# A fused linear layer with mean and condition terms on one core: first loads over one queue, tiles 4 to 7 turned by VectorE, bias added as banks are emptied, half the turned chunks in SBUF

## The chip, the cores and the metric

The kernel runs on one core of one Trainium2 chip. The time is device microseconds from start to end of one execution. Engines are named as in the profile: PE (TensorE, the matrix products), PEld (its weight loads), DVE (VectorE), ACT (ScalarE), POOL (GpSimd), SP (SyncE, which here only issues DMAs). A name with a q behind it (SPq, POOLq) is that engine's instruction queue.

## What is computed

The layer takes rows of x, the mean of x over the sequence and a condition vector used twice, multiplies all of them by one weight matrix, adds a bias, applies relu and adds x again. Shapes: x is (4, 1024, 512), the condition (4, 256), W (1536, 512), b (512), all float32.

```python
def _L0_cond_ref(hidden0, hidden1, x, W, b):
    hidden = jnp.concatenate([hidden0, hidden1], axis=-1)      # (B, 512)
    x_mean = jnp.mean(x, axis=1, keepdims=True)                # (B, 1, 512)
    ones_L = jnp.ones((1, L, 1), dtype=x.dtype)
    fused = jnp.concatenate([x, x_mean * ones_L, hidden[:, None, :] * ones_L], axis=-1)
    return jax.nn.relu(jnp.einsum('bld,do->blo', fused, W) + b)
x = x + _L0_cond_ref(cond_512, cond_512, x, L0_cond_W, L0_cond_b)
```

Only the x part of `fused` differs from row to row. The mean part and the condition part are the same for all 1024 rows of one batch entry, so the kernel computes them once per entry, together with b, as one 512-wide "bias".

## The kernel before

**Tiles.** The output has 32 tiles of 128 rows by 512 columns: eight tiles per batch entry r (the code calls an entry a row), numbered t = 0 to 31. One tile is one PSUM bank. Its product needs x with the contraction dimension on the partitions, so x is transposed ("turned") in chunks. The contraction of 512 is split into four parts j of 128.

**Three passes per product.** TensorE multiplies fp32r operands. To keep float32 accuracy, each turned chunk is split into a high part `hi` (ScalarE, L265, which also sums the chunk for the mean) and a low part `lo` (VectorE, L281); W is split in the same way into `w_hi` (L233) and `w_lo` (L235). `product(t, j)` (L459) issues three matrix products of 128 x 512: hi by w_hi, hi by w_lo, lo by w_hi. A tile takes 12 of them. The last tile is done in two halves of 256 columns, so that its second half overlaps the first one's end.

**Turning.** `units` (L156) groups tiles: tile 0, tile 1, tiles 2 and 3, tiles 4 to 7, then groups of four. Groups 0 to 3 (`TURN_PE`, the first entry) are turned by TensorE with an identity (L252) from x as loaded for the residual (L178). All later groups are turned by VectorE in 32 x 32 blocks (L254): the DMA brings x a second time as `z` (L191), four strided loads of 256 KB per group, laid out so that the block transposes give the full transpose. One piece is a group's chunk for one j (tiles 0 and 1: all j in one); there are 34 pieces. Turned pieces go to one of two PSUM banks (`ps_x`), their hi and lo parts to SBUF (`S_BUFS` = 15 pieces).

**The bias of an entry.** Sums over the sequence are added up (L336). Two condition terms are weighed by ScalarE (L348) and added by GpSimd (L353) into `cond`, starting from b times 1024 (L321). VectorE adds four mean terms in turn into `acc` in PSUM (L341), the first from `cond` in SBUF. `acc` is split into hi and lo (L357, L361), and two products with a matrix of 1/1024 (L373) sum over the partitions and spread the bias to all partitions of the bank `pb`.

**Getting the bias into a tile.** There are three ways. Tiles 0 to 2 (`KEEP`) are copied out by ScalarE before the bias is known (L473) and get it later by VectorE (L477). Tiles 3 to 15 (entries below `BY_PE` = 2) get it on TensorE: a product of a 64-row matrix `even` with the split bias `row` (L470) into the tile's bank, after which ScalarE's relu empties the bank (L480). Tiles 16 to 30 get it as VectorE empties the bank (L477), and relu follows in SBUF (L480). The last tile starts each half with two products that put its bias in (L455). GpSimd adds x (L485), and SyncE stores the tile (L497).

**What sets the order.** The schedule is manual. `Plan` holds every step with its cost per engine, its dependencies and an urgency; it places steps one by one at the earliest simulated start, and emits them in that order, so each engine's instruction order is fixed before launch, and an engine that waits holds up everything behind it on its queue. SyncE's loads and stores are in the same plan. The first loads are written out by hand (L198 to L211): x on SyncE, W's first block on ScalarE's queue, the condition and b on GpSimd's. Buffers: five banks for tiles, two for turned pieces, one for bias work; three z groups, four x groups, ten output tiles.

Of the kernel before, what the change touches and what calls it, by code (L numbers as in the profile page):

```python
# [1 line left out]

# [13 lines left out]
N_WARM = 11  # L16


class Plan:
# [5 lines left out]
    HANDOVER = 0.2  # L25
    PATIENCE = 0.1

    def __init__(self, engines):
        self.free = dict.fromkeys(engines, 0.0)
        self.todo, self.done, self.log = {}, {}, []  # L30

    def add(self, key, costs, deps, urgency, emit, later=0.0):


        assert key not in self.todo, key
        self.todo[key] = (costs, list(deps), urgency, emit, later)

    def run(self):
        while self.todo:
            could = []  # L40
            for key, (costs, deps, urgency, _, _) in self.todo.items():
                if not all(d in self.done for d in deps):
                    continue
                options = []
                for engine, cost in costs.items():
                    start = self.free[engine]
                    for d in deps:
                        end, later, by = self.done[d]
                        if by != engine:
                            end += later + self.HANDOVER  # L50
                        start = max(start, end)
                    options.append((start + cost, start, engine, cost))
                _, start, engine, cost = min(options)
                could.append((start, urgency, key, engine, cost))
            assert could, list(self.todo.items())[:8]
            first = min(could, key=lambda t: t[:2])
            start, _, key, engine, cost = min(
                (t for t in could if t[3] == first[3] and t[0] <= first[0] + self.PATIENCE),
                key=lambda t: (t[1], t[0]),
            )  # L60
            _, _, _, emit, later = self.todo.pop(key)
            self.log.append((start, engine, key, start - self.free[engine]))
            self.free[engine] = start + cost
            self.done[key] = (start + cost, later, engine)
            emit(engine)
# [512 lines left out]
```

## Time and profile before

| what | value |
|---|---|
| median of three runs | 117.61 us (117.05 to 119.56) |
| profiled execution: span | 115.7 us |
| moved by DMA | 26.31 MB, mean 227 GB/s (17.83 MB read, 8.39 MB written) |
| queue of SyncE (q1) | 25.17 MB, 75.7% of 16 engines' span |
| queue of ScalarE (q10) | 1.05 MB, 3.1% |

The profile shows one execution. In a timeline line the first number is the start and the second the duration, in us; brackets at its end hold the idle time before the instruction and what ended it. In a line of groups, "x30 | 38.7, 1315 | 38.9 <-ACT o" means 30 instructions, 38.7 us busy, 1315 ns each on average, 38.9 us idle before them, mostly ended by ScalarE's write to o. In the chain in order of time, each line is the start, the duration, the engine, the tile and line, and how many instructions were merged. In a table of stretches each line is the stretch, its length, and for each engine (PE, PEld, DVE, ACT, POOL) busy us and instruction count, then TensorE's granted clock as a share of full speed, the busy share of the DMA engines and GB/s. Matmul durations overlap, since they are pipelined: the spacing of starts is the cost.

### The profile page before, as it was taken

The page shows a single profiled execution, that of the slowest core. Times are in us where ns is not written, and L with a number is a line of the kernel's source. Part 1 is how long each engine was busy: PE and PEld are TensorE (multiplying, and loading weights), DVE is VectorE, ACT ScalarE, POOL GpSimd, SP SyncE. Part 2 cuts the span into 40 slices and gives each one's busy share as a digit, 9 for nine tenths or more (in the row PEclk, how much of TensorE's full clock was granted, in tenths as well). Part 3 has the DMA queues.
Part 4 walks back from the last instruction along what each step waited for, and adds up shares of the span by engine and source line. Part 5 has one row for each costly group of instructions (what it writes and reads, how often), then busy time and mean ns, then how long its engine had stood idle before and what let it go on. Part 6 is the DMA issues. An engine that isn't in the chain of part 4 may idle for free.

```text
span 115.7 us, 1477 instructions
## 1 busy us (share of the span) xinstructions
PE 107.7 (93%) x466; PEld 82.9 (72%) x466; DVE 81.0 (70%) x114; ACT 53.4 (46%) x122; POOL 57.8 (50%) x55
## 2 busy tenths in 40 slices
PE   5926999999999999999999999999999999999980
PEld 2415788888766687877766688887888878888870
DVE  1066734399999999976896999939999980632250
ACT  5055547887568460424963542246466140642200
POOL 6507144899809643040893029508354913199400
PEclk9998599999999999999999999999999999999999
DMA  3799999999999959999959999994422422025351
GB/s 109 179 392 396 394 370 198 203 203 205 205 256 281 199 136 207 304 388 390 349 177 213 272 397 407 400 258 176 164 91 106 169 91 91 0 91 222 140 227 45
DMA packets 22999, 26.31 MB, mean 227 GB/s; under 512 B 1228, under 2 KB 13776, under 8 KB 22864
## 3 DMA queue, kind: packets, MB, share of 16 engines
q1 hardware_dynamic: 22352, 25.17, 75.7%
q10 hardware_dynamic: 576, 1.05, 3.1%
q8 instruction: 3, 0.05, 0.2%
q14 instruction: 4, 0.03, 0.1%
q0 software_dynamic: 64, 0.01, 0.0%
HBM read 17.83 MB, written 8.39 MB: 227 GB/s over the span
## 4 chain that ended last, share of the span: by engine, by line
PE 89%; DMA 7%; SPq 1%; DVE 0%; issue 0%
PE po_None L459 77%; DMA x<-in_x_dram 7%; PE po_None L470 4%; PE xT L252 3%; PE po L459 2%; PE pb L373 2%; SPq L178 1%; PE po L455 0%; DVE o L490 0%; PE pt L324 0%
## 5 line engine op out<-in xcount | busy, mean ns | idle before, releaser
L485 POOL TENSOR_TENSOR o<-o,x 128x512 f32<-128x512 f32 x30 | 38.7, 1315 | 38.9 <-ACT o L480 32.1
L459 PE MATMUL po_None<-w_hi,hi 128*128 128x512 f32 x124 | 50.8, 409 | 0.0
L459 PE MATMUL po_None<-w_lo,hi 128*128 128x512 f32 x124 | 49.4, 398 | 0.0
L459 PE MATMUL po_None<-w_hi,lo 128*128 128x512 f32 x124 | 49.3, 398 | 0.0
L459 PEld LDWEIGHTS po_None<-w_hi,hi 128*128 128x128 f32 x124 | 23.5, 190 | 7.1 <-issue 1.6
L459 PEld LDWEIGHTS po_None<-w_hi,lo 128*128 128x128 f32 x124 | 23.6, 190 | 5.7
L459 PEld LDWEIGHTS po_None<-w_lo,hi 128*128 128x128 f32 x124 | 23.6, 190 | 5.0
L281 DVE TENSOR_TENSOR lo<-xT,hi 128x512 fp32r<-128x512 f32 (+1 forms) x34 | 21.9, 647 | 7.2 <-ACT hi L265 7.2
L254 DVE STREAM_TRANSPOSE xT<-z 128x512 f32<-128x512 f32 x24 | 26.2, 1102 | 0.3
L265 ACT ACTIVATE hi<-xT 128x512 fp32r<-128x512 f32 (+1 forms) x34 | 19.3, 571 | 9.3 <-DVE xT L254 5.5
L477 DVE TENSOR_TENSOR o<-po_None,bias 128x512 f32<-128x512 f32 x15 | 9.8, 677 | 12.2 <-ACT bias L379 4.1
L480 ACT ACTIVATE o<-o 128x512 f32<-128x512 f32 x17 | 10.5, 631 | 7.5 <-DVE o L477 7.5
L480 ACT ACTIVATE o<-po_None 128x512 f32<-128x512 f32 x13 | 7.5, 601 | 7.9 <-PE po_None L470 7.9
L341 DVE SCALAR_TENSOR_TENSOR acc<-w_mean,tot,acc 128x512 f32<-128x512 f32 x12 | 9.1, 756 | 0.4
L252 PE MATMUL xT<-ident,x 128*128 128x128 f32 x32 | 6.0, 307 | 3.5 <-DMA x<-in_x_dram 3.5
L252 PEld LDWEIGHTS xT<-ident,x 128*128 128x128 f32 x32 | 5.1, 207 | 4.6 <-issue 2.5
L357 ACT ACTIVATE acc_hi<-acc 128x512 fp32r<-128x512 f32 x4 | 2.4, 600 | 11.9 <-DVE acc L341 11.9
L265 ACT ACTIVATION_READ_ACCUMULATOR hi<-xT 128x1 f32 x32 | 6.4, 201 | 0.0
L353 POOL TENSOR_TENSOR cond<-bL,term 128x512 f32<-128x512 f32 x4 | 5.2, 1303 | 2.0 <-ACT term L348 2.0
L341 DVE SCALAR_TENSOR_TENSOR acc<-w_mean,tot,cond 128x512 f32<-128x512 f32 x4 | 5.7, 1426 | 0.6 <-POOL cond L353 0.3
L348 ACT ACTIVATE term<-wc,cT 128x512 f32<-128x512 f32 x8 | 5.6, 723 | 0.7 <-POOL cond L353 0.7
L353 POOL TENSOR_TENSOR cond<-cond,term 128x512 f32<-128x512 f32 x4 | 5.5, 1383 | 0.3
(54 smaller groups left out, 60.7 us busy)
## 6 DMA issues: line engine op xcount, KB each, us to landing
out_dram<-o SPq DMA_DIRECT2D x31, 256.0 KB, 2.4
x<-in_x_dram SPq DMA_DIRECT2D x7, 1024.0 KB, 7.9
z<-in_x_dram SPq DMA_DIRECT2D x24, 256.0 KB, 7.4
w_x<-in_L_cond_W_dram ACTq DMA_DIRECT2D x4, 256.0 KB, 7.2
w_cond<-in_L_cond_W_dram SPq DMA_DIRECT2D x1, 1024.0 KB, 12.7
w_mean<-in_L_cond_W_dram SPq DMA_DIRECT2D x1, 1024.0 KB, 12.6
x<-in_x_dram SPq DMA_DIRECT2D x2, 256.0 KB, 4.1
x<-in_x_dram SPq DMA_DIRECT2D x1, 512.0 KB, 8.0
```

Of the source, the lines that this page charges most:

```text
L252: nc.tensor.transpose(v[:, (m * n + i) * P : (m * n + i + 1) * P], x_t[:, j], ident)
L254: nc.vector.transpose(v[:, : n * P].rearrange("p (n t) -> p n t", t=Q), zs[u].rearrange("p n (a j) -> p n j a", j=J)[:, : n * NQ, js[0], :],)
L265: nc.scalar.activation(hi[c][:, :m], xT[c][:, :m], AF.Copy, accum_out=sums[:, r, js[0], s : s + 1] if len(js) == 1 else None,)
L281: nc.vector.tensor_tensor(lo[c][:, :m], xT[c][:, :m], hi[c][:, :m].bitcast(F32), ALU.subtract)
L341: nc.vector.scalar_tensor_tensor(acc[r], w_mean[:, j, :], totals[r][:, j : j + 1], acc[r] if j else conds[r], ALU.mult, ALU.add,)
L348: nc.scalar.activation(terms[r, k], wc[:, k], AF.Copy, scale=cT[:, k, r : r + 1])
L353: nc.gpsimd.tensor_tensor(conds[r], conds[r] if k else bL, terms[r, k], ALU.add)
L459: nc.tensor.matmul(pos[key][:, :w], lhsT=v[p][:, c], rhs=m[:, j, d], start=(h is None and j == 0 and n == 0), stop=((t < KEEP or r >= BY_P ...
L470: nc.tensor.matmul(pos[t], lhsT=even, rhs=rows[t // NK], start=False, stop=True)
L477: nc.vector.tensor_tensor(o, o if t < KEEP else pos[t], biases[t // NK], ALU.add)
L480: nc.scalar.activation(o_tile(t), pos[t] if KEEP <= t < BY_PE * NK else outs[t], AF.Relu)
L485: nc.gpsimd.tensor_tensor(outs[t], outs[t], x_tile(t), ALU.add)
```

## The change

The text is rewritten, but the tiles, the three passes and the path of the bias up to `pb` stay. What differs:

- **First loads**: SyncE issues all of them, in the order x0, W0, x1, W1, W2, W3, x of tiles 2 and 3, cond, b; `w_cond`, `w_mean`, the z groups and the x groups follow as the planner places them. W's first block uses a buffer of the x pool, which has five now.
- **Turning**: `BY_PE` = (0, 1, 2) now names the groups that TensorE turns, so tiles 4 to 7 are turned by VectorE from four more z loads. For groups that VectorE turns, the pieces of odd j are written to SBUF (`in_sbuf`), those of even j to PSUM as before; the low part of a piece in SBUF may be made by VectorE or GpSimd.
- **Bias**: no bias product per tile. Tiles 0 to 3 (`PARK`) are copied out and get the bias later (VectorE or GpSimd); tiles 4 to 30 get it as VectorE empties the bank; relu follows in SBUF for all of 0 to 29. The last tile starts each half with one 64-row product `preload` instead of two.
- **acc** starts with a ScalarE copy of `cond` into PSUM, so all four VectorE mean terms read `acc` from PSUM. Sums are scaled by 1/1024 in a tiny step of their own; b is no longer scaled.
- **Start of TensorE**: 5 warm-up products in place of 11, and `fill()` products of the same kind wherever the plan shows TensorE idle for over 0.35 us before the condition is turned. For tiles 0 to 3 (`FINE`) each of the three passes is a step of its own; a tile's parts j need only follow its first product, and not one another.
- **Planner**: due times are worked back from wanted ends; a step costs an occupancy and a latency per engine; loads and stores pass through one simulated DMA pipe; 240 noisy orders are simulated and the one with the shortest simulated end is emitted. `S_BUFS` is 14 (was 15), output buffers 12 (was 10).

```diff
-    S_BUFS = 15
-    X_BUFS = 4
-    O_BUFS = 10
-    TURN_PE = (0, 1, 2, 3)
-    BY_PE = 2
-    KEEP = 3
+    S_BUFS = 14
+    X_BUFS = 5
+    O_BUFS = 12
+    N_WARM = 5
+    PARK = 4
+    ALONE = NT - 2
+    FINE = 4
+    SEEDS = 240
...
+    BY_PE = (0, 1, 2)
+    def in_sbuf(c):
+        u, js = pieces[c]
+        return u not in BY_PE and js[0] % 2 == 1
...
+    first_loads = [
+        (("x", 0, 0), MB / 4, lambda e: load_x(0, 0, 1)),
+        (("w", 0), MB / 4, lambda e: load_w(0)),
+        (("x", 0, 1), MB / 4, lambda e: load_x(0, 1, 1)),
+        (("w", 1), MB / 4, lambda e: load_w(1)),
+        (("w", 2), MB / 4, lambda e: load_w(2)),
+        (("w", 3), MB / 4, lambda e: load_w(3)),
+        (("x", 0, 2), MB / 2, lambda e: load_x(0, 2, 2)),
+        (("c",), 0.05, lambda e: nc.sync.dma_start(out=c_sb, in_=cond)),
+        (("b",), 0.05, lambda e: nc.sync.dma_start(out=b_sb[0:1, :], in_=b.rearrange("(o d) -> o d", o=1))),
+    ]
...
     def turn(c):
-        v = xT[c] = ps_x.tile([P, G * P], F32, tag="x", name=f"xT{c}")
-        if u in TURN_PE:
+        if in_sbuf(c):
+            v = xT[c] = spool.tile([P, G * P], F32, tag="xs", bufs=2, name=f"xT{c}")
+        else:
+            v = xT[c] = ps_x.tile([P, G * P], F32, tag="x", name=f"xT{c}")
+        if u in BY_PE:
...
+        plan.add(("lo", c), {"dve": (a, a + 0.06)} | ({"pool": (1.3, 1.35)} if in_sbuf(c) else {}), [("hi", c)],
+                 lambda e, c=c: split_lo(e, c))
...
+    def acc_start(r):
+        acc[r] = ps_b.tile([P, D], F32, tag="b", name=f"acc{r}")
+        nc.scalar.activation(acc[r], conds[r], AF.Copy)
     def mean_term(r, j):
-        if not j:
-            acc[r] = ps_b.tile([P, D], F32, tag="b", name=f"acc{r}")
         nc.vector.scalar_tensor_tensor(
-            acc[r], w_mean[:, j, :], totals[r][:, j : j + 1], acc[r] if j else conds[r],
-            ALU.mult, ALU.add,
+            acc[r], w_mean[:, j, :], totals[r][:, j : j + 1], acc[r], ALU.mult, ALU.add
         )
...
-    def bias_to_bank(t):
-        nc.tensor.matmul(pos[t], lhsT=even, rhs=rows[t // NK], start=False, stop=True)
+    def preload(h):
+        nc.tensor.matmul(bank(LAST, h)[:, :HALF], lhsT=even, rhs=row["v"][:, columns(h)], start=True, stop=False)
...
+        if t < PARK:
+            plan.add(("freed", t), {"act": (0.49, 0.58)}, done + room, lambda e, t=t: keep(t), soft=chain)
+            plan.add(("biased", t), {"dve": (0.62, 0.68), "pool": (1.3, 1.35)}, [("freed", t), ("bias", r)],
+                     lambda e, t=t: add_bias(e, t))
+        elif t < ALONE:
+            plan.add(("freed", t), {"dve": (0.6, 0.66)}, done + room + [("bias", r)],
+                     lambda e, t=t: add_bias(e, t), soft=chain)
...
+    makespan, log, worst, how = plan.search(SEEDS)
+    pe_free, opened = 99.0, True
+    for s, e, key in log:
+        opened = opened and key[0] != "cT_pe"
+        if e == "pe":
+            if opened and s - pe_free > 0.35:
+                for _ in range(int((s - pe_free - 0.1) / 0.22)):
+                    fill()
+            pe_free = s + plan.tasks[key][0][e][0]
+        plan.tasks[key][2](e)
```

More of the change, by code (lines that the diff above doesn't have):

```diff
@@ L15 @@
 PSUM = bass.MemoryType.PSUM
-N_WARM = 11
 class Plan:
[L25 to L39, printed above, removed]
-            could = []
[L41 to L59, printed above, removed]
-            )
[L61 to L65, printed above, removed]
@@ L217 @@
[L217 to L226 removed]
+            deps = []
@@ new lines @@
+                key = ("product", t, j) + (("right",) if h else ())
+                cost = STEP if h is None else STEP / 2
+                plan.add(key, {"pe": (cost, cost + 0.17)},
+                         [("hi", c), ("lo", c), ("w_hi", j), ("w_lo", j)] + (first if not j else []),
+                         lambda e, t=t, j=j, h=h: product(t, j, h=h), due=due(t, j, 0, h or 0),
+                         soft=[key[:2] + (0,) + key[3:]] if j else chain)
+    for t in range(NT):
+        r, k = divmod(t, NK)
+        room = [("stored", t - O_BUFS)] if t >= O_BUFS else []
+        chain = [("freed", t - 1)] if t else []
+        done = [d for j in range(J) for d in made(t, j)]
```

540 lines of the change are left out of this document (304 added, 236 removed).

## The prediction

> **What bounds the kernel now.** I read the page's busy shares first, then the chain of work that ended last, then that chain in order of time, then stretches of the start, and last the queues of VectorE, GpSimd and SyncE.
>
> ```profile
> span 115.7 us, 1477 instructions
> PE 107.7 (93%) x466; PEld 82.9 (72%) x466; DVE 81.0 (70%) x114; ACT 53.4 (46%) x122; POOL 57.8 (50%) x55
> PE 89%; DMA 7%; SPq 1%; DVE 0%; issue 0%
> ```
> The chain is TensorE for 89% of the span: from its first product to its last no other engine holds the end. So an edit is worth what it takes out of TensorE's row of work, or out of the time before that row begins. The chain in order of time, then TensorE's timeline around one bias product:
>
> ```profile
> 15.37 0.71 PE xT L252 x6
> 17.48 0.47 PE xT L252 x4
> ...
> 33.34 0.90 PE po_None L470 x3
> 34.23 1.60 PE po_None L459 x6
> 35.83 0.42 PE po_None L470
> ...
> 54.35 1.35 PE po_None L470 x5
> ...
> 76.44 21.69 PE po_None L459 x93
> 98.13 0.45 PE pb L373 x2
> ...
> 112.40 0.02 issue
> 112.42 0.42 DVE o L490
> ```
> ```profile
> 38.86 0.40 PE L459 MATMUL po_None<-w_hi,lo 128*128 128x512 f32 x1
> 39.19 0.50 PE L470 MATMUL po_None<-row,even 64*128 64x512 f32 x1
> 39.62 0.50 PE L459 MATMUL po_None<-w_hi,hi 128*128 128x512 f32 x1
> 39.96 0.40 PE L459 MATMUL po_None<-w_lo,hi 128*128 128x512 f32 x1
> ```
> A product of 512 columns costs 21.69/93 = 0.233 us, a transpose 0.47/4 = 0.117. A bias product standing alone costs more than a product: from 38.86 to 39.96 lie two products and one bias product, so it takes 1.10 - 2 x 0.233 = 0.63 us, since TensorE loses time on both sides of the 64-row operand. The end is 112.42, and 3.3 us follow it (a VectorE step and the last store).
>
> The start, by stretches of 5 us (their last columns are granted clock, DMA share, GB/s), then its timeline:
>
> ```profile
> 0.00:5.00 5.00, 3.81 (x12) 1.59 (x13) 0.35 (x3) 1.49 (x2) 3.38 (x13) 1.00 0.50 122
> 5.00:10.00 5.00, 1.52 (x11) 1.17 (x10) 2.67 (x5) 2.23 (x4) 1.11 (x1) 1.00 1.03 378
> 10.00:15.00 5.00, 5.00 (x20) 3.85 (x20) 3.39 (x8) 2.57 (x8) 1.43 (x2) 0.66 1.07 401
> 20.00:25.00 5.00, 5.00 (x25) 4.13 (x24) 3.10 (x4) 4.64 (x10) 4.30 (x4) 1.00 1.22 204
> ```
> ```profile
> 0.74 1.87 SPq L178 DMA_DIRECT2D x<-in_x_dram  x4
> 1.20 3.90 PE L144 MATMUL pw<-warm 128*128 128x512 bf16 x11 [1.20 <-DVE ones L137]
> 4.93 0.64 PE L252 MATMUL xT<-ident,x 128*128 128x128 f32 x4
> 6.66 0.63 ACT L233 ACTIVATE w_hi<-w_x 128x512 fp32r<-128x512 f32 x1 [4.43 <-DMA w_x<-in_L_cond_W_dram]
> 7.20 0.58 ACT L265 ACTIVATE hi<-xT 128x512 fp32r<-128x512 f32 x1
> 7.33 0.69 DVE L235 TENSOR_TENSOR w_lo<-w_x,w_hi 128x512 fp32r<-128x512 f32 x1 [1.02 <-ACT w_hi L233]
> 10.04 0.48 PE L459 MATMUL po_None<-w_hi,hi 128*128 128x512 f32 x1
> 16.00 2.54 POOL L332 TENSOR_TENSOR wc<-w_cond 128x512 f32<-128x512 f32 x2 [3.98 <-DMA w_cond<-in_L_cond_W_dram]
> ```
> The first quarter of W is there only at 6.66 and products begin at 10.04, with x, W and w_cond sharing the transfers. TensorE then stays busy 102.4 us (10.04 to 112.4), of which (1 - 0.66) x 5 = 1.7 us go to a clock granted at half after the sparse stretch before.
>
> **The change part by part.**
>
> *First loads in order of need.* Nine go through SyncE: 256 KB each for x0, W0, x1, W1, W2, W3, then 512 KB of x, then cond and b; w_cond and w_mean come behind. At 1.87/4 = 0.47 an issue, W0's starts at 1.2 as it does now from ScalarE, and the ninth is out by 5.0, ahead of the data; GpSimd's two small issues, now SyncE's, were off the path and stay so. By the rows 0.61 MB have passed at 5.0 and 0.378 MB more in each us after. W0 is complete after 0.52 MB, about 4.4. How late the landing is seen has no row of its own: zero below; above, w_cond's 4.19 MB had passed at about 14.2 and were used at 16.00, so 1.8. I take 0.8, nearer the lower end, as fewer loads run side by side: W0 at 5.2. With 0.63 for w_hi and some 0.15 of handovers, products begin at **6.0** (5.2 with no lag; 7.5 if W0 lands at 6.66 as now).
>
> *New waits there.* W1 (1.05 MB) is seen at 7.0, so its w_hi serves at 7.6. Until then TensorE has three products of tile 0 and four transposes, 1.2 us less their own waits, for 1.6 us: about **0.9** us stand idle (0 to 2), tile 1 being late too. W3 (1.57 MB, 8.3) is usable at 9.7 while TensorE has work until about 12, so it costs nothing. Tile 1's transposes now lie behind the first product: +0.5.
>
> *Five warm-up products for eleven.* 3.90/11 = 0.355 each, so they end near 3. The planner may add some in gaps. The loss to half clock is 1.7 now; it may be 0 or the same 1.7; I take 0.8, between. The Trainium skill, page "TensorE: Matmul & The Clock Gate", section "Part 1: The HAM clock gate", says that the full clock is granted only after a busy window of about 3.4 us. By that rule five would not do, the sum would be 0.9 higher, and the time 109.1, inside the forecast's own range; no run yet shows it.
>
> *Tiles 4 to 7 by VectorE.* Sixteen transposes leave TensorE: -16 x 0.117 = -1.9. Four strided x loads (1.05 MB) are added; the row 20 to 25 shows such loads at 204 GB/s, 5.1 us. Behind 2.1 MB (9.0) they end at 14.1, seen at 14.9; TensorE is busy with tiles 0 to 3 (48 products, 12 transposes) until 6.0 + 0.9 + 0.8 + 11.2 + 1.4 = 20.3, so the first turned chunk (turn 1.1, high part 0.6, low part 0.65, handovers: 2.6, ready at 17.5) has 2.8 us to spare. If w_cond and w_mean go ahead (2.1 MB, 5.3 us), that cover is gone and 2.5 us are lost.
>
> *Bias added as banks are emptied.* The 13 bias products go: five alone at 0.63, the three in 0.90 and the five in 1.35 with about 0.2 behind each group (six products in 1.60 where 1.40 is usual): 3.1 + 1.1 + 1.55 = **-5.8**. For the last tile two 64-row products replace four half ones: between -0.2 and +0.8, I take +0.3. VectorE gets the work:
>
> ```profile
> L321 DVE TENSOR_SCALAR bL<-b_sb 128x512 f32<-128x512 f32 x1 | 0.9, 905 | 0.0
> L485 POOL TENSOR_TENSOR o<-o,x 128x512 f32<-128x512 f32 x30 | 38.7, 1315 | 38.9 <-ACT o L480 32.1
> L254 DVE STREAM_TRANSPOSE xT<-z 128x512 f32<-128x512 f32 x24 | 26.2, 1102 | 0.3
> L281 DVE TENSOR_TENSOR lo<-xT,hi 128x512 fp32r<-128x512 f32 (+1 forms) x34 | 21.9, 647 | 7.2 <-ACT hi L265 7.2
> L477 DVE TENSOR_TENSOR o<-po_None,bias 128x512 f32<-128x512 f32 x15 | 9.8, 677 | 12.2 <-ACT bias L379 4.1
> L341 DVE SCALAR_TENSOR_TENSOR acc<-w_mean,tot,acc 128x512 f32<-128x512 f32 x12 | 9.1, 756 | 0.4
> L341 DVE SCALAR_TENSOR_TENSOR acc<-w_mean,tot,cond 128x512 f32<-128x512 f32 x4 | 5.7, 1426 | 0.6 <-POOL cond L353 0.3
> ```
> VectorE: 81.0 + 4 turns (4.4) + 13 more additions (31 for 18, 8.8) - 4 x 0.67 (ScalarE now writes acc's first term, 2.7) - 1.3 for small ones (bL's scaling and one low part of a bias row, less four scalings of sums) = **90.2**, of which GpSimd can take up to 14 low parts. ScalarE gains about 3 (four first terms and one more copy at 0.6) on 53.4, and has room.
>
> *Half the chunks turned into SBUF.* The turn itself has no row with that target: I take the 1.102 of the turn into PSUM, the same operation. What is new is that their low part reads two SBUF tensors. The timeline shows what such an instruction does beside GpSimd:
>
> ```profile
> 43.18 1.29 POOL L485 TENSOR_TENSOR o<-o,x 128x512 f32<-128x512 f32 x1 [1.49 <-ACT o L480]
> 43.22 1.82 DVE L341 SCALAR_TENSOR_TENSOR acc<-w_mean,tot,cond 128x512 f32<-128x512 f32 x1
> ```
> VectorE's step with w_mean and cond, both in SBUF, takes 1.82, ending 0.57 behind GpSimd's; its twelve sisters with acc in PSUM take 0.756. Over the four the excess is 1.426 - 0.756 = 0.67 each. The change removes these four and brings 14 low parts that VectorE or GpSimd (about 1.3 each) may do. The Trainium skill, page "SBUF — State Buffer", section "Who interferes with whom", says that a VectorE instruction with two SBUF inputs and a GpSimd one that reads SBUF exclude each other for a whole instruction; the trace agrees (1.82 against 0.756), and the rule speaks against this part. At half of them on VectorE: 7 x 0.67 = 4.7, with 7 x 0.65 moved off: VectorE stays near 90 in some 104. No engine exceeds TensorE then, but VectorE's idle share falls from 30% to some 13%. The waits of TensorE that follow have no row: zero below, as now; above, 5 (the second rival's price). I take **1.5**, nearer zero because GpSimd, 50% busy, can take low parts. This is the least certain term.
>
> *New planner.* Each queue still runs one fixed order; SyncE's matters most:
>
> ```profile
> SPq L497 <- POOL o L485: 46.6, 21, 5.5
> 58.48 2.04 SPq L191 DMA_DIRECT2D z<-in_x_dram  x4
> ```
> Stores wait for GpSimd 21 times, 46.6 us, up to 5.5; what stands behind them waits too. The last z group now goes at 58.48, before most stores. With one group more and the same three buffers that order tightens. By bytes it fits: 2.1 MB to 9.0, seven z groups 36, two weight blocks 5.3, four x groups and 16 stores 10.6 each give 71.5, and the last group (tiles 28 to 31) is needed near 84: 103.0 less its four tiles' products 11.2, four turns 4.4 and a bias chain of about 6, plus one tile's 2.8, since the bias frees a bank only for the second of them. I cost it at nothing beyond the 1.5.
>
> **The sum.** TensorE's row: 102.4 - 1.9 - 5.8 + 0.5 + 0.3 - 1.7 + 0.8 + 0.9 + 1.5 = 97.0. From 6.0 it ends at 103.0; with 3.3 behind it the span is 106.3. The profiled execution's 115.7 stands 1.9 below the median 117.61 of the three runs; the same added gives **108.2**.
>
> **The rivals.**
> *Nothing waits.* First product at 5.2, full clock, no idle at the start, none later: 108.2 - 0.8 - 0.8 - 0.9 - 1.5 = 104.2. TensorE's almost gapless row now speaks for it; three queues filled above 80% speak against.
> *VectorE becomes the bound through the shared reading.* All 14 low parts on VectorE at 0.67 extra: 90.2 + 9.4 = 99.6, of which some 6.4 fall before 15 (the rows of the three first stretches); the rest, run without a gap from 15, ends at 108.2, and with 3.3 and 1.9 that is 113.4. That the planner may choose GpSimd speaks against. It is the rule of the Trainium skill's page "SBUF — State Buffer" carried to its end.
> *Slower: loads behind stores.* If SyncE's order puts z groups behind stores that wait for GpSimd, a group comes late by up to the 5.5 shown, and nothing else turns the next chunk. Three late groups not covered by chunks in store give 108.2 - 1.5 + 16.5 = 123.2; it decides from about 4.5 us each (over 120). Speaking against it: up to 14 chunks, over three groups, can be held ahead.
> *The loads gain nothing by their order.* Products begin at 7.5: 109.7, inside the likeliest case's own range.
>
> **How the numbers follow.** 0.47 for the forecast (own range 106 to 110), 0.18 for nothing waits (104 to 106), 0.17 for VectorE as bound (110 to 115.2), 0.07 for a mixture ending within 2% (115.3 to 120, about what a measurement of this kernel can tell from no change), 0.11 for slower, most of it loads behind stores. Faster 0.82, same 0.07, slower 0.11. The range 104.0 to 114.0 leaves out the last two and a little of the third.
>
> **What would show it.** The first product near 6.0 and no half clock beyond 11; no 64-row products before the last tile; the chain still TensorE, in one row of about 97 us; low parts from SBUF on VectorE over 1 us where GpSimd runs. It is wrong if TensorE stands for several us together, waiting for a turned chunk (z late, or VectorE full) or for a bank (bias late).

## The result and the profile after

The changed kernel takes 112.35 us (median of four runs, 111.12 to 116.24) against 117.57 us; the ratio is 0.9443 with a 95% interval of 0.9361 to 0.9526, so it is 5.6% faster. The median holds two longer executions, which the ratio leaves out on both sides. Measured once more (e12 below), the ratio is 0.9584 (0.9486 to 0.9683); the gain is thus 4 to 6%. The profiled execution took 111.12 us with a span of 109.3, 1.8 beside the span.

The page of the changed kernel: span, busy time of each engine, and the chain that ended last by engine.

```profile
span 109.3 us, 1441 instructions
PE 102.1 (93%) x432; PEld 77.4 (71%) x432; DVE 88.8 (81%) x125; ACT 57.0 (52%) x126; POOL 68.6 (63%) x61
PE 60%; DVE 15%; DMA 9%; POOL 7%; ACT 4%; issue 2%; SPq 1%; DVEq 0%; POOLq 0%
```

TensorE held 89% of the chain before and holds 60% now; VectorE, GpSimd and transfers have the rest. The chain in order of time shows where they have it.

```profile
25.87 0.77 DVE acc L444
...
41.50 2.51 POOL o L559 x2
...
44.12 5.29 DMA out_dram<-o
...
49.45 1.29 DVE o L553 x2
...
50.78 20.56 PE po_None L538 x87
71.34 0.47 PE pb L459 x2
71.82 20.99 PE po_None L538 x90
92.81 0.46 PE pb L459 x2
...
106.24 0.42 DVE o L564
```

From 50.78 to 106.2 TensorE works without a gap. Before that it is released by others, at 50.78 by VectorE's bias addition (L553), which empties a bank. The chain names a store (the DMA at 44.12) as what VectorE waited for at 49.45, but VectorE had no idle time there: its two parked additions run from 47.68 for 2.45 us (shown under e1). Ahead of 49.45 the stretches are therefore a better guide than the chain. The busy times by stretches of the changed kernel (columns: length, PE, PEld, DVE, ACT, POOL, each with its instructions, then granted clock, DMA share, GB/s) say why.

```profile
0.00:5.00 5.00, 3.82 (x11) 1.75 (x12) 0.80 (x4) 1.49 (x2) 2.12 (x10) 1.00 0.56 137
...
10.00:15.00 5.00, 5.00 (x26) 3.83 (x25) 1.54 (x5) 1.92 (x6) 0.57 (x1) 1.00 1.21 203
15.00:20.00 5.00, 5.00 (x24) 4.09 (x23) 3.88 (x6) 2.76 (x10) 1.71 (x2) 1.00 1.02 392
20.00:25.00 5.00, 4.84 (x19) 2.90 (x18) 4.75 (x7) 4.66 (x10) 4.39 (x4) 1.00 1.23 197
30.00:35.00 5.00, 4.87 (x21) 3.31 (x20) 5.00 (x8) 3.31 (x11) 1.80 (x2) 1.00 1.18 220
40.00:50.00 10.00, 8.48 (x35) 6.05 (x33) 9.79 (x14) 4.47 (x10) 8.97 (x8) 1.00 1.20 240
```

VectorE, 1.54 of 5 us busy between 10 and 15, is busy for 29.3 of the 30 us from 20 to 50, and between 40 and 50 TensorE has gaps while VectorE has 0.2 us free. The start of the changed kernel, in the timeline of all engines:

```profile
1.18 2.31 PE L195 MATMUL pw<-warm 128*128 128x512 bf16 x5 [1.18 <-DVE one L185]
5.35 0.63 ACT L315 ACTIVATE w_hi<-w_x 128x512 fp32r<-128x512 f32 x1 [3.13 <-DMA w_x<-in_L_cond_W_dram]
5.89 0.58 ACT L357 ACTIVATE hi<-xT 128x512 fp32r<-128x512 f32 x1
6.17 1.13 PE L344 MATMUL xT<-ident,x 128*128 128x128 f32 x4 [0.38 <-DMA x<-in_x_dram]
6.95 0.64 PE L538 MATMUL po_None<-w_hi,hi 128*128 128x512 f32 x1
```

W's first quarter is used at 5.35 (before: 6.66) and the first product begins at 6.95 (before: 10.04). Two fixed orders stand between W and that product: ScalarE makes w_hi before the high part of tile 0 (5.89), and tile 1's transposes (6.17), which wait for x1, lie ahead of the first product.

VectorE's groups of the changed kernel (busy us, mean ns):

```profile
L346 DVE STREAM_TRANSPOSE xT<-z 128x512 f32<-128x512 f32 x28 | 29.0, 1086 | 0.0
L553 DVE TENSOR_TENSOR o<-po_None,bias 128x512 f32<-128x512 f32 x27 | 17.6, 679 | 5.3 <-POOL o L559 3.6
L373 DVE TENSOR_TENSOR lo<-xT,hi 128x512 fp32r<-128x512 f32 (+1 forms) x26 | 18.9, 734 | 4.8 <-ACT hi L357 4.8
L437 DVE TENSOR_SCALAR tot<-tot 128x4 f32<-128x4 f32 x4 | 3.4, 856 | 0.1
```

The turns cost what they did (1.09), into SBUF or PSUM. The low parts' mean of 0.73 hides two kinds: 0.64 to 0.69 alone (0.42 for the four of half the size), and 0.92 to 1.58 for five, where both operands lie in SBUF and GpSimd runs. The surprise is L437: scaling four columns takes 0.86.

### The profile page after: what moved, and what is told of

The parts are those of the page before. It is cut to its first block, busy times and chain, and to the rows that moved or that the text cites. A ratio compares the mean times of both kernels' runs of the same rounds, so it can differ in the third digit from the quotient of the medians.

```text
span 109.3 us, 1441 instructions
## 1 busy us (share of the span) xinstructions
PE 102.1 (93%) x432; PEld 77.4 (71%) x432; DVE 88.8 (81%) x125; ACT 57.0 (52%) x126; POOL 68.6 (63%) x61
## 4 chain that ended last, share of the span: by engine, by line
PE 60%; DVE 15%; DMA 9%; POOL 7%; ACT 4%; issue 2%; SPq 1%; DVEq 0%; POOLq 0%
PE po_None L538 53%; DVE xT L346 7%; DMA out_dram<-o 5%; POOL o L559 5%; DMA x<-in_x_dram 4%; DVE lo L373 3%; PE po L538 3%; ACT hi L357 2%; DVE acc L444 2%; PE xT L344 2%; DVE o L553 1%; POOL lo L373 1%; POOL o L553 1%; DVE tot L437 1%; PE pb L459 1%
## 5 line engine op out<-in xcount | busy, mean ns | idle before, releaser
L346 DVE STREAM_TRANSPOSE xT<-z 128x512 f32<-128x512 f32 x28 | 29.0, 1086 | 0.0
L556 ACT ACTIVATE o<-o 128x512 f32<-128x512 f32 x30 | 18.2, 630 | 9.7 <-DVE o L553 9.3
L373 DVE TENSOR_TENSOR lo<-xT,hi 128x512 fp32r<-128x512 f32 (+1 forms) x26 | 18.9, 734 | 4.8 <-ACT hi L357 4.8
L553 DVE TENSOR_TENSOR o<-po_None,bias 128x512 f32<-128x512 f32 x27 | 17.6, 679 | 5.3 <-POOL o L559 3.6
L444 DVE SCALAR_TENSOR_TENSOR acc<-w_mean,tot,acc 128x512 f32<-128x512 f32 x16 | 12.1, 754 | 0.6
L373 POOL TENSOR_TENSOR lo<-xT,hi 128x512 fp32r<-128x512 f32 x8 | 10.4, 1299 | 2.6 <-ACT hi L357 2.6
L421 POOL TENSOR_TENSOR wc<-w_cond 128x512 f32<-128x512 f32 x2 | 2.5, 1295 | 7.7 <-DMA w_cond<-in_L_cond_W_dram 7.7
L430 POOL TENSOR_TENSOR cond<-b_sb,term 128x512 f32<-128x512 f32 x4 | 5.6, 1404 | 0.5 <-ACT term L425 0.5
L430 POOL TENSOR_TENSOR cond<-cond,term 128x512 f32<-128x512 f32 x4 | 5.6, 1412 | 0.2
L320 POOL TENSOR_TENSOR w_lo<-w_x,w_hi 128x512 fp32r<-128x512 f32 x1 | 1.7, 1674 | 6.0 <-DVE w_hi L317 6.0
L463 ACT ACTIVATE bias<-pb 128x512 f32<-128x512 f32 x4 | 2.4, 596 | 5.4 <-PE pb L459 5.4
```

The source lines that it names most:

```text
L346: nc.vector.transpose(v[:, : n * P].rearrange("p (n t) -> p n t", t=Q), zs[u].rearrange("p n (a j) -> p n j a", j=J)[:, : n * NQ, js[0], :],)
L373: nc_of[e].tensor_tensor(lo[c][:, :m], xT[c][:, :m], hi[c][:, :m].bitcast(F32), ALU.subtract)
L421: nc.gpsimd.tensor_tensor(wc[:, k], w_src["cond"][:, 0, k], w_src["cond"][:, 1, k], ALU.add)
L430: nc.gpsimd.tensor_tensor(conds[r], conds[r] if k else b_sb, terms[r, k], ALU.add)
L444: nc.vector.scalar_tensor_tensor(acc[r], w_mean[:, j, :], totals[r][:, j : j + 1], acc[r], ALU.mult, ALU.add)
L553: nc_of[e].tensor_tensor(o, o if t < PARK else bank(t), biases[t // NK], ALU.add)
```

## The experiments

"Order kept" means that the planner's order is the changed kernel's and only single steps are edited; e4 to e7 let the planner search again. All ratios are to the kernel before on the same chip, with 95% intervals. TensorE's waits are told by the starts of neighbouring products, less 0.233 for the first.

**e1: the four scalings removed.** 1/L goes into the matrix that spreads the sums, and cond and b are taken times L. Order kept.

```diff
-    nc.gpsimd.memset(ones32, 1.0)
+    nc.gpsimd.memset(ones32, 1.0 / L)
...
-        nc.vector.tensor_scalar(totals[r], totals[r], 1.0 / L, None, ALU.mult)
+        pass
```

> The changed kernel with its order of instructions kept, but without the four 4-column scalings of the sums (the scale is put into the spreading matrix, b and the condition instead, as in the kernel before). In the changed kernel these four take 0.58 to 1.06 us each, each beside a GpSimd instruction. Theory A (VectorE is full from 17 to 50 us and loses about 4 us there to GpSimd through shared reading of SBUF): two of the four, 1.6 us, lie before the wait for a bank at 48.9 to 50.8, which shrinks by 1 to 1.6; time 1.0 to 1.6 below the changed kernel's 111.1. Theory B (VectorE is full because it was given more work, the sharing costs nothing that counts): four steps of 0.12 us are gone, time within 0.4 of 111.1.

First VectorE's timeline of the changed kernel over the stretch in question, then GpSimd's there, then VectorE's in e1, and e1's chain behind it.

```profile
42.20 0.58 DVE L437 TENSOR_SCALAR tot<-tot 128x4 f32<-128x4 f32 x1
42.81 2.34 DVE L444 SCALAR_TENSOR_TENSOR acc<-w_mean,tot,acc 128x512 f32<-128x512 f32 x3
...
47.68 2.45 DVE L553 TENSOR_TENSOR o<-o,bias 128x512 f32<-128x512 f32 x2
```
```profile
47.69 1.29 POOL L430 TENSOR_TENSOR cond<-b_sb,term 128x512 f32<-128x512 f32 x1
```
```profile
41.30 2.34 DVE L446 SCALAR_TENSOR_TENSOR acc<-w_mean,tot,acc 128x512 f32<-128x512 f32 x3
...
46.17 2.90 DVE L555 TENSOR_TENSOR o<-o,bias 128x512 f32<-128x512 f32 x2
```
```profile
49.72 22.11 PE po_None L540 x87
```

The chain that makes the second batch entry's bias (three of its four mean terms in 2.34) begins 1.51 earlier in e1 (41.30 for 42.81), and TensorE's wait for the bank ends at 49.72 for 50.78, 1.06 earlier. The two parked additions (o and bias, both in SBUF) take 2.45 for two beside GpSimd's addition, and 2.90 in e1: each operation that comes earlier meets GpSimd elsewhere. The 87 products behind the wait, which are 20.56 in the changed kernel, took 22.11 here, since the clock granted from 50 to 60 was 0.83: the longer wait before them lost more than was won. That holds for this execution; another, at a clock of 1.00, took 110.15 us, 1.0 below the changed kernel's 111.12, as theory A expects. The time is 111.56 us, ratio 0.9547 (0.9287 to 0.9807), the profiled span 109.8. So the scalings do delay the bias, but 1 us on the chain gave no gain that the runs resolve.

**e2: GpSimd's additions of x become fills, which read nothing.** The output then holds neither the products nor x. Order kept.

```diff
-        nc.gpsimd.tensor_tensor(outs[t], outs[t], x_tile(t), ALU.add)
+        nc.gpsimd.memset(outs[t], 0.0)
+        nc.gpsimd.memset(outs[t], 0.0)
+        nc.gpsimd.memset(outs[t][:, :P], 0.0)
```

> The changed kernel with its order kept; GpSimd's 30 additions of x are replaced by three fills of the output tile (512, 512 and 128 columns, about 1.3 us together), which read nothing from SBUF. So the output lacks the products and x. Theory A: VectorE's low parts and bias additions with two SBUF inputs fall to 0.65 to 0.7 wherever the additions of x were their partner, the waits of TensorE between 40 and 51 shrink by 1 to 2 us; time 109 to 110. Theory B: no instruction of VectorE gets shorter, time within 0.5 of 111.1.

VectorE's timeline of e2 at a scaling, then GpSimd's there:

```profile
68.13 0.61 DVE L437 TENSOR_SCALAR tot<-tot 128x4 f32<-128x4 f32 x1
```
```profile
68.19 0.53 POOL L559 MEMSET o<- 128x512 f32 x1 [0.91 <-ACT o L556]
```

113.0 us (110.79 to 115.26), ratio 0.9549 (0.9508 to 0.959). The profile is of an execution of 115.03 us, so its durations are read, not its waits. After 50 us VectorE's low parts all take 0.64 to 0.69 here, where the changed kernel has one of 1.05 (at 57.66) and one of 1.58 (at 74.50): their lengthening there does come from GpSimd's additions of x. But the time did not fall to the 109 to 110 of theory A, for the stretch that matters was not freed. GpSimd's term additions (L430) and its two parked additions stay: before 40 us three low parts still take 1.07 to 1.26 and a scaling 1.07, and the two parked additions keep a mean of 1.23. And the fills themselves hold up a scaling, though they read nothing: the one above ends at 68.74, the fill at 68.72. So what the shared port costs in time stays open.

**e3: the two fixed orders of the start swapped.** Tile 0's high part goes ahead of w_hi, tile 1's transposes behind the first product. Order kept elsewhere.

```diff
+    move(("hi", 0), ("turn", 0))
+    move(("turn", 1), ("product", 0, 0, 0))
```

> The changed kernel; only two steps change their place: ScalarE makes the high part of x0 before that of W0, and TensorE issues its first product before tile 1's transposes. Theory A: the 0.95 us between the forecast first product (6.0) and the measured one (6.95) is the fixed order, with which both engines wait for a later load first; the first product starts at about 6.1 and the time falls by 0.3 to 0.9, less if VectorE's full stretch swallows it. Rival: the loads alone set the start; first product at 6.6 or later and no change beyond 0.2.

TensorE's timeline of e3, first product and wait for the bank:

```profile
6.27 0.51 PE L538 MATMUL po_None<-w_hi,hi 128*128 128x512 f32 x1 [0.81 <-ACT w_hi L315]
...
50.87 0.50 PE L538 MATMUL po_None<-w_hi,hi 128*128 128x512 f32 x1 [1.54 <-DVE o L553]
```

The first product comes 0.68 earlier, the bank at 50.87 as before (50.78), the span is 109.4, ratio 0.9621 (0.9418 to 0.9824). What TensorE gains at its start it waits for at 50: the time to there is not TensorE's.

**e4: the planner's next seeds.**

```diff
-        for seed in range(seeds):
+        for seed in range(seeds, 2 * seeds):
```

> The changed kernel with the next 240 seeds of the planner's search, so with another order of the same work. Theory A: VectorE's full stretch is there in any order of this work; PE waits 3 to 6 us in all, time 110 to 113. Rival: the waits belong to this one order; another order moves the time by over 2 us either way and puts the waits elsewhere.

115.34 us, ratio 0.9743 (0.9631 to 0.9855), span 111.6; the median is above the 110 to 113 of theory A. The waits stand elsewhere, as the rival has it: 1.02 at 22 (for a GpSimd low part), 0.60 at 37, 1.87 at 40.4 (for the bias addition), 0.93 at 71.5. So it is no fault of one order: another order has waits of the same kinds, here more of them. Its span is 2.3 us above that of the changed kernel and 1.7 above that of e12 (109.9), but the intervals of its ratio and of e12's overlap.

**e5: the kernel before, with the bias added by VectorE alone.**

```diff
-    BY_PE = 2
+    BY_PE = 0
```

> The kernel before with one part of the change alone: no bias products per tile; tiles 0 to 2 get the bias later, tiles 3 to 30 as VectorE empties the bank. The prediction's step: TensorE loses 5.8 us of products. Theory A (VectorE is the limit between 25 and 50 us already in the kernel before, busy 4.9 of 5 there, and 13 more additions of 0.68 lie mostly in that stretch): TensorE waits for banks or turned chunks and gives back 3 us or more; time 114 to 117. Rival: the additions fit beside the rest; TensorE's row shortens by the 5.8 and the time is 111.5 to 112.5.

```profile
36.96 0.47 PE L459 MATMUL po_None<-w_hi,hi 128*128 128x512 f32 x1 [0.84 <-DVE o L477]
...
47.39 0.50 PE L459 MATMUL po_None<-w_hi,hi 128*128 128x512 f32 x1 [1.80 <-DVE o L477]
```

These rows are TensorE's timeline of e5; the kernel before waits at neither place. Its time is 115.87 us, ratio 0.9867 (0.9797 to 0.9936), span 114.2 for 115.7. So of the 5.8 us priced for the bias, some 1.5 arrive. The rest returns as waits of 1.01 and 1.96 and half clock behind them (0.89 in the stretch 50 to 60), which in this execution comes in place of the half clock of the start. The old text's VectorE is full too where TensorE waits (9.79 of the 10 us from 40), though idle a fifth of its time overall.

**e6: tiles 4 to 7 turned by TensorE again.**

```diff
-    BY_PE = (0, 1, 2)
+    BY_PE = (0, 1, 2, 3)
```

> The changed kernel with tiles 4 to 7 turned by TensorE again (the planner makes its own order for it). The prediction's step: 16 transposes, 1.9 us, come back to TensorE. Theory A: VectorE loses 4 turns (4.1 us) in its full stretch, TensorE's waits before 52 us fall from 5 to 2 or less, so the time does not rise: 109.5 to 111. Rival (the part is worth its transposes, the waits are the order's): 112.5 to 113.5. Another order of the same work has been 2.3 longer, so the waits in the trace count more than the time.

The same view by stretches, e6:

```profile
15.00:20.00 5.00, 5.00 (x29) 4.36 (x28) 1.50 (x4) 2.81 (x10) 1.34 (x2) 1.00 1.10 265
20.00:25.00 5.00, 5.00 (x28) 3.97 (x26) 2.18 (x6) 2.14 (x6) 0.00 (x0) 1.00 1.23 205
...
50.00:60.00 10.00, 8.88 (x39) 6.84 (x38) 10.00 (x12) 6.82 (x16) 9.79 (x8) 1.00 0.36 139
```

114.74 us, ratio 0.9697 (0.9591 to 0.9802), span 112.6: the expectation that fewer turns on VectorE would give 109.5 to 111 missed. VectorE is idle for 6.3 of the 10 us from 15 to 25, as its first z is for later tiles (seen only at 25.75), then from 85 to 100% busy to 80, and TensorE waits 1.22 at 34.7, 1.29 at 50.6 and 1.35 at 72. So in this order the time that the turns of tiles 4 to 7 leave on VectorE stays empty, and its full stretch is no easier for it. The new search is mixed into the size of this, and the interval of the ratio overlaps e12's.

**e7: all chunks turned into PSUM.**

```diff
-        return u not in BY_PE and js[0] % 2 == 1
+        return False
```

> The changed kernel with all chunks turned into PSUM (own order). No low part reads two SBUF tensors, none can go to GpSimd. Theory A (VectorE's amount of work in the stretch counts, and turning into SBUF helps by letting GpSimd take eight low parts, 5.4 us, at a price of 2.7 us of waiting for the shared reading): VectorE's busy time 90 to 92, time 112 to 114. Rival (the shared reading costs more than GpSimd takes): VectorE's waits before 52 fall, time 109 to 110.5.

VectorE's groups in e7, turns and scalings:

```profile
L346 DVE STREAM_TRANSPOSE xT<-z 128x512 f32<-128x512 f32 x28 | 30.6, 1105 | 6.3 <-DMA z<-in_x_dram 5.9
L437 DVE TENSOR_SCALAR tot<-tot 128x4 f32<-128x4 f32 x4 | 0.7, 170 | 0.1
```

116.28 us, ratio 0.9826 (0.9707 to 0.9946). No shared reading lengthens a low part here (mean 0.673) and the scalings cost 0.17, yet it is slower, and slower than both expectations (112 to 114, 109 to 110.5), with VectorE busy for 87.7 and not 90 to 92: VectorE waits 5.9 us for z (not at all in the changed kernel) and TensorE once 3.46 for a low part. The profile is of an execution of 119.14 us, so the waits are read by their kind. By the ratios turning into SBUF is worth 2.8 to 4.5 us in this text (against e12 and against the first measurement) in spite of its price, with a new search in that figure; that it is by chunks held ahead fits the waits for z and was not tried by itself.

**e8: W's four loads on ScalarE's queue.** Order kept.

```diff
-        nc.sync.dma_start(out=w_src["x"][:, j, :], in_=Wv[0, :, j])
+        nc.scalar.dma_start(out=w_src["x"][:, j, :], in_=Wv[0, :, j])
```

> The changed kernel with its order kept; only W's four first loads are issued on ScalarE's queue again. The prediction's step: one queue in order of need brings W0 earlier. Theory A: with two queues W0 shares the transfers with x; its high part starts at 6.2 or later (5.35 now), the first product at 7.5 or later, and yet the end stays within 0.5 of 111.1, because TensorE later waits for VectorE anyway. Rival 1: the landing does not depend on the queue (5.3 to 5.5). Rival 2: each us lost at the start is lost at the end.

ScalarE's timeline, VectorE's, and the last wait for a bank in TensorE's, all of e8:

```profile
6.61 0.63 ACT L315 ACTIVATE w_hi<-w_x 128x512 fp32r<-128x512 f32 x1 [4.38 <-DMA w_x<-in_L_cond_W_dram]
...
11.03 0.63 ACT L315 ACTIVATE w_hi<-w_x 128x512 fp32r<-128x512 f32 x1 [1.99 <-DMA w_x<-in_L_cond_W_dram]
```
```profile
18.02 0.42 DVE L373 TENSOR_TENSOR lo<-xT,hi 128x256 fp32r<-128x256 f32 x1 [4.06 <-ACT hi L357]
...
21.36 3.10 DVE L346 STREAM_TRANSPOSE xT<-z 128x512 f32<-128x512 f32 x3
```
```profile
55.29 0.50 PE L538 MATMUL po_None<-w_hi,hi 128*128 128x512 f32 x1 [1.56 <-DVE o L553]
```

115.29 us, ratio 0.9796 (0.9715 to 0.9877). W's first quarter is used at 6.61 (5.35), a later one only at 11.03, and everything behind is shifted by about 4.5, of which up to 1.7 is a half clock of TensorE (0.50 from 12 to 15) behind its wait for W: the first turn comes at 21.36 (16.88), the bank at 55.29 (50.78). The theory that the end stays where it is, as the first 50 us are VectorE's, fell. VectorE's first turn stands in its fixed order behind low parts of the last TensorE-turned tile, those wait for ScalarE's high parts, and these for the tile's transposes in TensorE's row, which waits for W: so VectorE's full stretch begins when W lets it, and z is no longer what it waits for. (In e3 the first turn is at 16.97: only the first product came earlier there, W's last quarters did not.) By the ratios one queue in order of need is worth 2.5 to 4.1 us (against e12 and against the first measurement).

**e9, e10, e11: versions meant to beat the changed kernel; e12: the changed kernel again, on the same chip.** e11 does one thing: VectorE's turn of piece 7, the second chunk of tiles 4 to 7, goes ahead of two low parts. e10 takes e1's edit and moves the parked bias additions behind the additions that free banks 8 to 10. e9 does all of e1, e3, e10 and e11.

```diff
+    move(("turn", 7), ("lo", 3))
...
+    move(("biased", 2), ("freed", 10))
+    move(("biased", 3), ("biased", 2))
```

> The changed kernel with its order kept but for these moves: no scalings of the sums (as in the run without them), the high part of x0 and the first product ahead, the turn of the second chunk of tiles 4 to 7 ahead of two low parts for which VectorE waits, and the two late bias additions of tiles 2 and 3 behind the additions that empty the banks of tiles 8 to 10. Theory A (the end is set by when VectorE begins its full stretch and by what stands in it ahead of the bias of the second batch entry): the wait for a bank near 49 us shrinks from 1.7 to 0.3 or less, TensorE's waits fall from 5.7 to 3 or less; 1.5 to 2.5 below the changed kernel of the same call. Rival: VectorE stays full, the wait comes back at the next entry's bias (near 71) or as a late low part; within 0.7 of the changed kernel.

> Two of those edits alone: no scalings of the sums, and the two late bias additions behind the three that empty banks. Theory A: the bank of tile 8 is emptied at 47.9 to 48.5 (50.8 in the changed kernel, 49.7 with the scalings gone alone); the wait falls to 0 to 0.3; 1.2 to 2 below the changed kernel of the same call. Rival: something else than these additions holds the bank (bias not ready): wait over 1 us.

> One edit alone: the turn of tiles 4 to 7's second chunk (into SBUF, so no PSUM bank is needed) stands ahead of the low parts of two chunks of tiles 2 and 3, for which VectorE waits 1.1 and 0.5 us. Theory A (the full stretch of VectorE begins late because the turn stands behind these low parts, not because z lands late): the turn starts at 15.6 or earlier (16.9 now), the wait near 49 shrinks by 0.7 to 1.1. Rival: z lands at about 16.5 only, the turn starts there, and the low parts behind it make TensorE wait 1 us near 17.

> The changed kernel unchanged, on the same chip as the three others, for their comparison. Its runs so far went from 111.1 to 116.2: if the spread comes with stretches of TensorE at half clock behind its long waits, the runs with a mean granted clock of 1.0 lie near 111 and those at 0.98 near 113.

VectorE's timeline of e11, then of e9, at the first turn; then VectorE's and TensorE's of e9 further on:

```profile
16.17 1.08 DVE L346 STREAM_TRANSPOSE xT<-z 128x512 f32<-128x512 f32 x1 [1.44 <-DMA z<-in_x_dram]
```
```profile
17.59 1.08 DVE L346 STREAM_TRANSPOSE xT<-z 128x512 f32<-128x512 f32 x1 [2.17 <-DMA z<-in_x_dram]
...
50.56 1.89 DVE L555 TENSOR_TENSOR o<-po_None,bias 128x512 f32<-128x512 f32 x3 [1.46 <-ACT bias L465]
```
```profile
64.32 0.79 PE L540 MATMUL po_None<-w_hi,lo 128*128 128x512 f32 x1 [1.96 <-POOL lo L373]
```

In e11 the first z is there only at 16.2, as its rival expects, so a turn put earlier waits 1.44, the low parts behind it make TensorE wait 1.07, and the wait for the bank stays at 1.69. In e9 and e10 the bank's wait shrinks from 1.70 to 0.88, not to 0.3 or less: with the scalings gone and the parked additions moved, VectorE itself waits for ScalarE's copy of the bias (1.46 in e9, 2.22 in e10). What was won comes back further on: TensorE waits 2.13 in e9 (at 61.97) and 2.14 in e10 (at 66.13) for a low part that GpSimd makes, as the rival of e9 has it.

Medians and ratios: e9 117.06, 0.9721 (0.962 to 0.9822); e10 115.88, 0.9641 (0.9506 to 0.9777); e11 113.16, 0.9646 (0.9562 to 0.973); e12 114.64, 0.9584 (0.9486 to 0.9683). By the ratios none is better than the unchanged e12, so the gains of 1.2 to 2.5 us that were expected did not come. The changed kernel has less than a microsecond in its z's arrival (first turn at 16.88), and in the profiles of all three versions VectorE waits for z instead of working earlier (1.44 in e11, 2.17 in e9, 4.4 in e10, whose profile is of an execution of 118.06 us).

Of e12's six executions the three with a clock near 1.0 took 111.66 to 112.80, as expected, but the three at 0.967 to 0.985 took 116.48 to 118.25, not 113. Half clock accounts for 1.7 to 3.8 us of that (1 less the clock, times the span); the rest is open.

## Why the prediction came out as it did

Faster, by a chain that is TensorE's in its second half: that was right. The time forecast was 108.2 us in a range of 104 to 114, the median 112.35, above the likeliest case's own range of 106 to 110 and in the part that the prediction gave to VectorE as the bound (110 to 115.2, at 0.17). The median of e12, 114.64, would have lain outside the range. Against the profiled execution, by the prediction's own sum:

| step | forecast | measured |
|---|---|---|
| first product | 6.0 | 6.95 |
| TensorE's row, waits left out | 93.8 | 94.1 |
| idle and half clock at the start of the row | 0.9 + 0.8 | 0.4 |
| waits later | 1.5 | 4.8 |
| behind the last product | 3.3 | 3.1 |
| span | 106.3 | 109.3 |

The row without waits is the measured row, 109.3 - 3.1 - 6.95 = 99.3, less 5.2: the distances between starts in excess of 0.233 a product and 0.117 a transpose where the excess is 0.09 or more, without the last tile's preloads, which are in the 93.8.

*The step that was mis-sized* is "I take 1.5, nearer zero because GpSimd can take low parts", called the least certain term. It measured 4.8. Of it 1.70 is the bank at 48.85, 0.92 a low part at 44.65, two are of 0.32 and 0.31, and the other 1.6 lies in steps of about 0.1, mostly behind such waits. The reason given for the value failed: GpSimd took 8 of the 34 low parts, but VectorE was still full from 20 to 50. The prediction took some 90 us in about 104 and read 13% idle; the page has 88.8, so the total was right. But of the 20.5 us that VectorE was idle some 10 lie before 17, where its next work had not come, and 10 behind 90. The changed kernel is a milder form of the second rival (113.4): VectorE binds to 50.8, TensorE from there. That the shared reading makes it bind, as the rival has it, is not shown.

*Loads in order of need.* W0 was forecast at 5.2 and used at 5.35; e8 shows the order to be worth 2.5 to 4.1 us. The first product came 0.95 later than forecast since the prediction did not follow ScalarE's and TensorE's queue orders there (so its 0.5 for tile 1's transposes fell ahead of the row) and since TensorE was at half speed until then (tile 1's four transposes take 0.78, where the row has 0.47); e3, where it comes at 6.27, shows that this costs nothing at the end.

*Half clock.* 0.8 was taken. The column of the granted clock reads 1.00 in every stretch of the changed kernel, but the trace has a record of the clock only from 7.32 on, and before that the spacing tells another story:

```profile
4.30 1.49 PE L195 MATMUL pw<-warm 128*128 128x512 bf16 x3
```

Each of these starts (1.49 - 0.64)/2 = 0.43 behind the other, as the first five do, where the last of the kernel before are 0.22 apart from 4.07 on (its record begins at 3.97). So TensorE ran at half speed until about 7.3. Nearly all of that lies ahead of the row; the row lost 0.25, at the first product, whose successor starts 0.48 behind it. That the row lost no more is not so in every execution: in e2, with the same start, TensorE stands idle for 0.99 ahead of 6.78 (0.38 ahead of 6.17 here), and half clock follows from 9.03 to 12.44. The Trainium skill, page "TensorE: Matmul & The Clock Gate", section "Part 1: The HAM clock gate", wants a busy window of about 3.4 us. The five warm-ups take 2.31, and by that rule alone the prediction took them as too few; but transposes and three more warm-ups keep TensorE busy for 3.82 of the first 5 us. The rule is not contradicted; the count of warm-ups was the wrong thing to hold against it.

*Tiles 4 to 7 on VectorE.* The 1.9 us off TensorE held. z was forecast at 14.9 and lands at about 16.2 (e11): of the 2.8 us to spare 1.3 went to z, 0.7 to the low parts ahead of the turn (16.88), and the rest to two more turns that VectorE makes before the first low part (at 19.87); a wait of 0.32 at 20.03 is all that followed.

*Bias.* The 64-row bias products were priced at 5.8, and the spacing around all 13 in the kernel before gives 5.8 too. That they leave TensorE is right, but e5 shows them alone to bring only 1.5: "31 additions for 18" was counted as VectorE's total, not as where they fall. The mean terms, the parked additions and the second entry's bias meet in the stretch in which VectorE also turns every chunk.

*Half the chunks in SBUF.* The turn at 1.1 is right (1.09). The excess of 0.67 for each low part on VectorE was too much: the 26 low parts took 18.9, and without blocking 22 of 0.67 and four of 0.42 would take 16.4, so 2.5 us in all against 4.7. But the prediction priced only the low parts. The two parked additions on VectorE paid 1.2, and the four scalings 3.4 - 4 x 0.17 = 2.7, so 6.4 in all. The Trainium skill, page "SBUF — State Buffer", section "Who interferes with whom", counts tensor_scalar among the operations that can take the port shared with GpSimd, and says that whoever issues first holds it for a whole instruction. The prediction used this page for instructions with two SBUF inputs alone; these rows agree with the wider rule:

```profile
24.00 1.74 POOL L430 TENSOR_TENSOR cond<-b_sb,term 128x512 f32<-128x512 f32 x1
```
```profile
24.70 1.06 DVE L437 TENSOR_SCALAR tot<-tot 128x4 f32<-128x4 f32 x1
```

GpSimd's addition (first fence, the changed kernel) ends at 25.74, VectorE's scaling of four columns (second) at 25.76. In e6, with GpSimd idle from 20 to 25, the same step takes 0.17. The scaling of e2 that ends with a fill, which reads nothing, agrees with it as well.

*Loads behind stores*, the slower rival: SyncE still waits for GpSimd before stores, but VectorE does not wait for z in the changed kernel; the price did not come. In e9, e10 and e11 VectorE does wait for z, but no store stands ahead of those loads (SyncE's first stores go at 43.55 and later), so these waits are not this rival's.

The parts do not add up: without the one queue 2.5 to 4.1 us are lost, without SBUF 2.8 to 4.5, without the turns 1.3 to 3.0 (by the ratios, against e12 and the first measurement, the last not clear of noise), and the bias alone brings 1.5, while the whole gives 4.9 to 6.5. In e6, e7 and e8 TensorE meets a full or late VectorE at another place each time.

What stays open is how much of the 4.8 us of waits would go with the shared reading alone (e2 did not free the stretch), what an earlier bias would bring in e9 and e10, and what part of e4, e6 and e7 is the planner's new search. No version here is measurably better than the changed kernel.

## What to carry to other kernels

When work moves from the bounding engine to another, lay the receiver's work out by stretches and ask where the moved work falls: an engine idle 30% of the span can be full in the very stretch that takes it, and then part of the gain, most of it in e5, comes back as waits. Test each part of a combined change by itself, since parts that feed one chain neither add up nor stay in place. In a written-out order, a gain ahead of a wait on another engine is swallowed by that wait, so look at the last wait's release before mending the start, and at what would release it next: in e9 and e10 the bias took over where the parked additions had stood.

## What the runs showed of the hardware

A step of 128 x 4 on VectorE with all operands in SBUF took 0.58 to 1.06 us beside GpSimd in the changed kernel, and 0.17 where GpSimd was idle: a small instruction pays what is left of its neighbour's time. In e2 the neighbour was a fill, which reads nothing, and the step took 0.61. GpSimd pays too, 1.74 for an addition of 1.29. The turn, whose mean is 1.09 with half of the chunks going to SBUF, showed no such lengthening.

A single wait of TensorE in a full row can bring the half clock back. In e1 2.15 us were lost at 47.34 to 49.72, and the granted clock (in the view by stretches, TensorE's alone) fell behind it:

```profile
50.00:52.00 2.00, 2.00 (x6) 0.53 1.23 206
52.00:54.00 2.00, 2.00 (x7) 0.62 1.15 267
54.00:56.00 2.00, 2.00 (x10) 1.00 1.06 407
```

e5 shows the same behind 1.96 (0.50 from 50 to 52), e9 behind 2.13 and e10 behind 2.30 (0.50 from 46.9 to 50.3). Behind 1.70 in the changed kernel and 1.87 in e4 the clock stayed at 1.00, and so it did behind a second wait of e10, 2.14 at 66.13. So the length of the wait alone does not decide. The granted clock changes only in steps of 3.41 us in each trace (half clock lasts from 50.11 to 53.53 in e1, from 46.90 to 50.32 in e10). Laid out on these steps, the time lost within one of them was 2.0 to 2.3 us in the four cases in which the clock fell, and 1.7 or less where it did not; e10's second wait is cut by the step at 67.4 into 1.0 and 1.1. That is worked out from these few waits and was not tried by itself. The Trainium skill, page "TensorE: Matmul & The Clock Gate", section "Part 1: The HAM clock gate", names an idle window of about 3.4 us for the fall; here about 2 us of idle time were enough, and the measurement decides. In e1 the half clock took 1.6 us on top of the wait (22.11 for 20.56).
